# A hand-held issue order of 2640 steps, exchanged for another order of the same steps

## The chip, the cores and the metric

The kernel runs on one core of one Trainium2 chip. The metric is the device time of one execution in microseconds (us), the median over several runs; lower is better.

## The reference

The inputs are 16 batches of 256 query tokens x and 256 context tokens y, 256 features each, all in float32. Three attention layers with 16 heads of 16 features and one MLP are applied to every batch:

```python
# layer 0: cross attention with RMS norms, mask over the context
Q, K, V = rms(x, g_q) @ Wq, rms(y, g_c) @ Wk, rms(y, g_c) @ Wv      # by heads
x = rms(x + softmax(where(mask, Q K^T * scale, -inf)) V @ Wo, g_out)
# layer 1: causal self attention, layer norm, rotary turn of q and k
h = ln(x);  x = x + softmax(causal(rope(q) rope(k)^T)) v @ sa_wo + sa_bo
# layer 2: cross attention, q from ln(x), k and v from y, rotary turn
x = x + softmax(rope(q) rope(k)^T) v @ ca_wo + ca_bo
# MLP with 1024 hidden features
x = x + gelu(ln(x) @ fc1 + b1) @ fc2 + b2
```

## The kernel before

Work is cut into 48 attentions, one for each batch and layer. The list ORDER gives the layer of each: attentions 0 to 4 belong to layer 0, then the layers are mixed, and the last ones are of layer 2, so that batches are at different layers at the same time. Class Att holds the pieces of one attention as small methods; class Mlp holds those of the MLP for two batches. The methods are generators: each call goes to the next yield. A string PLAN lists which piece goes on next, and its order is the order in which instructions are put into the in-order queues of all engines:

```python
def step(word):
    if word not in steps:
        steps[word] = begin(word) or iter(())
    next(steps[word], None)
...
for word in PLAN.split():
    step(word)
```

A word is a method, the number of the attention and, for scores and values, a part. A word that stands three times is a generator in three stages. What the words mean, with lines as in the profile:

- `q.i`, `k.i`, `v.i`, `project.i`: a dense product of 32 column-tiled matmul records (L635 or L647) into one of three PSUM banks (tile d). The second stage reads the bank: DVE L796 (times rq, layer 0), ScalarE L762 (bias, layers 1 and 2), DVE L1076 or L1082 for project. For v the second stage is a small POOL instruction and the third the DVE read (L921 or L930). In layers 1 and 2 four further stages on DVE turn q and k (L770, L776 twice, an add).
- `k_high`, `k_low`, `k_out` and `q_high`, `q_low`, `q_out`: in layers 0 and 2 from attention 2 on ("fast"), q and k are split into two halves of float32r; k_high is ScalarE L877, q_high ScalarE L825, the low parts are DVE L881, L832 and L836, and the out steps are DMAs of SP (L889, L842).
- `scores.i.n`: the first stage is the matmuls (L966 fast, L955 else) into both buffers of tile S; the second and third are the two exponentials on ScalarE (L978), which free the two buffers. A causal attention has two more stages, masks on POOL (L986).
- `values.i.n`: the product with va into the single PSUM tile A (L1009); where a half of the heads is finished a second stage copies it (ScalarE, L1024). `take_last.i` is the copy of the last half.
- `heads_in`, `sums_in`, `invert` (three stages: DVE reciprocal, DMA to DRAM, DMA back), `divide` (POOL, then DVE L1069): the way from the copied result to `project`.
- `stats_x`, `stats_y`, `stats`, `norm`: normalization on DVE with a root on POOL. `send.i` and `receive.i` take the row factors of x through DRAM to tile rq (L719, L726 on SP). `pieces` and `pieces_in` turn a normalized batch through DRAM (L594, L600), `turn` does it with TensorE (L570).
- `load.b`, `load_early.n` (SP), `load_piece.b.n`, `load_later.n` (GpSimd's queue): loads of inputs and weights; load_early.0 is the first third of ca, 256 KB.
- `fold_of_att`, `fold_of_fc1`, `gain_*`, `combine.n`: work on the weights. `mlp.g.*`: the first MLP steps; mlp.0.up2 is a product whose PSUM result ScalarE copies (L1245).

The scores stage that sets how close two steps can stand:

```python
pss = [psS.tile([P, 2, 512], F32, tag="S", name="S") for g in range(2)]   # psS has 2 buffers
...                                      # 16 matmuls, alternating between the two tiles
for ps in pss:
    yield
    nc.scalar.activation(pt[:, :, :w], ps[:, :, :w], AF.Exp, scale=scale)
```

Before the plan a short written prologue runs attention 0's first products; after it, from about 672 us on, a written loop over the eight MLP groups runs to the end. Both are outside the string.

Of the kernel before, what the change touches and what calls it, by code (L numbers as in the profile page):

```python
# [55 lines left out]
scores.0.1 stats_x.2 values.0.0 q.1 scores.0.2 stats_y.2 v.1 scores.0.2 stats_y.2 scores.0.2  # L56
stats_x.3 values.0.1 load_piece.5.0 scores.0.3 stats_x.2 k.1 scores.0.3 stats_x.3 send.2 stats_y.3
scores.0.3 k.2 v.1 load_piece.5.1 v.1 send.2 k.1 values.0.1 send.3
scores.1.0 k_high.2 k_low.2 load_early.4 q.2 scores.1.0 send.3 scores.1.0 values.0.2 receive.2
load_early.3 scores.1.1 k_out.2 values.0.3 scores.1.1 q.3 q.2 scores.1.1 take_last.0 load_early.0  # L60
q_high.2 scores.1.2 q_low.2 values.1.0 scores.1.2 q_low.2 heads_in.0 v.2 v.2 stats_y.6 scores.1.2
q_out.2 scores.1.3 v.2 sums_in.0 k.3 stats_x.6 scores.1.3 receive.3 scores.1.3 load.4 values.1.1
k_high.3 values.1.1
scores.2.0 invert.0 values.1.2 k_low.3 scores.2.0 q.3 values.1.3 scores.2.0 heads_in.0 take_last.1
q_high.3 scores.2.1 invert.0 v.3 v.3 k_out.3 q_low.3 stats_x.6 scores.2.1 q_low.3 sums_in.1
scores.2.1 stats_y.3 values.2.0 stats_x.4 scores.2.2 stats_x.4 q_out.3 k.4 scores.2.2
load_piece.6.0 send.4 v.3 send.4 scores.2.2 load_piece.5.3 values.2.1 send.6 divide.0 k_high.4
stats_y.4 scores.2.3 invert.0 q.4 invert.1 scores.2.3 k_low.4 scores.2.3 receive.4 invert.1
stats_x.8 values.2.1
scores.3.0 heads_in.1 stats_x.8 values.2.2 scores.3.0 heads_in.1 fold_of_att load_piece.6.1  # L70
scores.3.0 q.4 load_early.2 load_later.1 values.2.3 divide.0 stats_y.4 q_high.4 invert.1
scores.3.1 send.8 take_last.2 project.0 scores.3.1 q_low.4 k_out.4 q_low.4 scores.3.1 values.3.0
project.0 fold_of_att q_out.4 scores.3.2 project.0 v.4 v.4 divide.1 scores.3.2 stats_y.8 project.0
scores.3.2 values.3.1 load_piece.5.2 finish.0 fold_of_att load_piece.7.2 scores.3.3 stats.5
values.3.1 k.6 scores.3.3 v.4 stats.5 scores.3.3 values.3.2 load_piece.7.0 sums_in.2 norm.5
k_high.6
scores.4.0 load_piece.7.1 k_low.6 values.3.3 scores.4.0 divide.1 fold_of_att turn.5 take_last.3
scores.4.0 send.6 project.1 fold_of_att turn.5 sums_in.3 invert.2 scores.4.1 heads_in.2 divide.2
project.1 load_later.0 q.5 project.1 scores.4.1 heads_in.2 fold_of_att project.1 scores.4.1
values.4.0 invert.2 invert.3 q.5 load_piece.6.2 scores.4.2 finish.1 heads_in.3 k.5 scores.4.2 q.5  # L80
q.5 load_early.1 scores.4.2 invert.3 values.4.1 q.5 receive.6 k.5 q.5 scores.4.3 k_out.6
values.4.1 q.6 k.5 q.5 q.5 invert.2 k.5 scores.4.3 v.5 v.5 stats_y.6 k.5 scores.4.3 k.5 heads_in.3
load_piece.6.3 values.4.2 q.6 stats.7
scores.5.0 q_high.6 values.4.3 stats.7 q_low.6 scores.5.0 v.6 q_low.6 scores.5.0 take_last.4
scores.5.0 q_out.6 divide.2 scores.5.0 send.8 scores.5.1 v.5 divide.3 v.6 norm.7 project.2
invert.3 scores.5.1 pieces.7 scores.5.1 pieces.7 scores.5.1 values.5.0 sums_in.4 project.2
scores.5.2 project.2 scores.5.1 k.8 v.6 scores.5.2 project.2 divide.3 pieces_in.7 scores.5.2
scores.5.2 values.5.1 finish.2 k_high.8 scores.5.2
scores.6.0 values.5.1 heads_in.4 project.3 load_later.6 stats.9 scores.6.0 load_piece.7.3 k_low.8
scores.6.0 stats.9 values.5.2 invert.4 stats_y.10 load_later.4 invert.4 scores.6.1 load_later.9  # L90
take_last.5 q.7 scores.6.1 norm.9 keep.5 pieces.9 scores.6.1 values.6.0 project.3 divide.4
sums_in.5 q.7 scores.6.2 project.3 pieces.9 k.7 q.7 scores.6.2 heads_in.4 project.3 q.7 scores.6.2
invert.4 values.6.1 q.7 q.7 scores.6.3 heads_in.5 q.7 v.7 k.7 invert.5 invert.5 divide.5
scores.6.3 k.7 receive.8 v.7 load_piece.9.0 heads_in.5 q.8 q.7 k.7 stats_y.8 values.6.1 k.7
scores.6.3 invert.5 values.6.2 k.7 divide.4 k_out.8
scores.7.0 v.7 project.4 stats_x.10 scores.7.0 pieces_in.9 q.8 scores.7.0 scores.7.0 values.6.3
project.4 q_high.8 load_piece.8.1 scores.7.1 divide.5 load_later.5 q_low.8 project.5 stats_x.10
scores.7.1 q_low.8 take_last.6 q_out.8 scores.7.1 scores.7.1 v.8 project.5 sums_in.6 stats.11
scores.7.0 scores.7.2 project.4 stats.11 q.9 scores.7.2 heads_in.6 scores.7.1 norm.11 scores.7.2
values.7.0 scores.7.2 pieces.11 q.9 values.7.1 load_piece.8.2  # L100
scores.8.0 pieces.11 q.9 values.7.1 v.8 k.10 scores.7.2 invert.6 scores.8.0 heads_in.6
load_later.8 q.9 scores.8.0 keep.9 q.9 values.7.2 k_high.10 invert.6 v.8 load_piece.8.0 scores.8.1
stats_y.10 take_last.7 scores.8.1 k.9 q.9 sums_in.7 scores.8.1 q.9 project.4 gain_ca values.8.0
k.9 finish.3 scores.8.2 send.10 v.9 v.9 k.9 divide.6 send.10 scores.8.2 load_later.7 k_low.10
invert.6 scores.8.2 invert.7 values.8.1 k.9 q.9 pieces_in.11 scores.8.3 k.9 values.8.1 k.11
finish.4 scores.8.3 receive.10 k.9 invert.7 scores.8.3 k_out.10 values.8.2 v.9 k.11 stats_x.14
scores.9.0 k.11 heads_in.7 stats_x.14 q.10 scores.9.0 k.11 load_later.10 invert.7 divide.6
scores.9.0 values.8.3 scores.9.0 q.10 heads_in.7 divide.7 scores.9.1 k.11 load_later.3 q_high.10
k.11 scores.9.0 project.6 scores.9.1 take_last.8 load_piece.9.1 q_low.10 k_high.11 sums_in.8 v.10
v.10 scores.9.1 stats.13 scores.9.1 q_low.10 scores.9.1 values.9.0 project.6 q_out.10 scores.9.2  # L110
send.14 divide.7 stats.13 heads_in.8 q.11 k_low.11 scores.9.2 load_piece.10.0 norm.13 heads_in.8
scores.9.2 scores.9.2 invert.8 project.7 v.10 q.11 keep.7 invert.8 q.11 values.9.1 scores.9.2
k_out.11
scores.10.0 q.11 values.9.1 k.12 scores.10.0 q.11 project.7 scores.10.0 values.9.2 q.11 invert.8
stats.12 q_high.11 scores.10.1 heads_in.9 v.11 v.11 take_last.9 stats.12 scores.10.1 pieces.13
sums_in.9 scores.10.1 q_low.11 values.10.0 norm.12 k.12 scores.10.2 pieces.13 q_low.11 keep.12
turn.12 stats.16 q_out.11 scores.10.2 fold_of_fc1 load_piece.8.3 v.11 heads_in.9 scores.10.2
values.10.1 divide.8 k.12 stats.16 turn.12 scores.10.3 invert.9 values.10.1 divide.8 q.12 divide.9
scores.10.3 k.12 pieces_in.13 k.12 scores.10.3 values.10.2 k.12 invert.9 q.12
scores.11.0 stats_y.14 project.8 q.12 scores.11.0 q.12 scores.11.0 values.10.3 q.12 fold_of_fc1  # L120
k_high.12 q.12 scores.11.1 fold_of_fc1 take_last.10 k.13 scores.11.1 k_low.12 invert.9 project.8
scores.11.1 k_out.12 values.11.0 q_high.12 scores.11.2 v.12 v.12 q_low.12 fold_of_fc1 scores.11.2
q_low.12 scores.11.2 divide.9 q_out.12 values.11.1 norm.16 k.13 scores.11.3 project.6 heads_in.10
project.9 scores.11.3 k.13 project.6 send.14 k.13 values.11.1 load_later.2 scores.11.3 k.14
sums_in.10 k.13 stats_y.14 project.9 k.13
scores.12.0 load_piece.10.1 v.12 values.11.2 scores.12.0 gain_fc1.0 stats.15 values.11.3
scores.12.0 pieces.16 k_high.14 receive.14 scores.12.1 pieces.16 k_low.14 q.13 scores.12.1
heads_in.10 stats.15 take_last.11 project.8 scores.12.1 keep.11 values.12.0 sums_in.11 invert.10
q.13 scores.12.2 load_piece.10.2 invert.10 q.13 values.12.1 scores.12.2 divide.10 q.13 v.13 v.13
heads_in.11 scores.12.2 q.13 q.13 values.12.1 heads_in.11 scores.12.3 q.13 q.13 norm.15 q.14  # L130
invert.10 scores.12.3 pieces.15 scores.12.3 finish.6 pieces.15 values.12.2 k_out.14 q.14
scores.13.0 invert.11 stats_x.17 divide.11 k.15 invert.11 scores.13.0 stats.19 pieces_in.15
scores.13.0 scores.13.0 values.12.3 v.13 q_high.14 stats.19 scores.13.1 k.15 stats_x.17 q_low.14
v.14 scores.13.1 divide.10 q_low.14 scores.13.1 scores.13.1 take_last.12 project.10 k.15 q_out.14
# [1932 lines left out]
```

## Time and profile before

| | |
|---|---|
| median of 3 runs | 880.16 us (880.13 to 881.4) |
| the profiled execution's own time | 880.08 us |
| its span, first to last instruction | 878.4 us |
| instructions | 32887 |
| busy: PE, PE weight load, DVE, ACT, POOL | 99%, 64%, 75%, 68%, 40% |
| DMA: bytes, mean rate | 107.04 MB, 122 GB/s |
| granted TensorE clock | 1.000 |

PE is TensorE, PEld its weight loads, DVE VectorE, ACT ScalarE, POOL GpSimd, SP the engine that issues most DMAs. A line of the timeline gives the start in us, the length in us, engine, line, operation, the tile written and those read, and the number of records merged; in brackets stand the idle time before and what ended it. A line of the waits gives who waited for whom, the total in us, how often, and the longest. The busy time of PE is modelled at its end, so a wait of a few tenths of a microsecond can lie hidden in it.

### The profile page before, as it was taken

The page shows a single profiled execution, that of the slowest core. Times are in us where ns is not written, and L with a number is a line of the kernel's source. Part 1 is how long each engine was busy: PE and PEld are TensorE (multiplying, and loading weights), DVE is VectorE, ACT ScalarE, POOL GpSimd, SP SyncE. Part 2 cuts the span into 40 slices and gives each one's busy share as a digit, 9 for nine tenths or more (in the row PEclk, how much of TensorE's full clock was granted, in tenths as well). Part 3 has the DMA queues.
Part 4 walks back from the last instruction along what each step waited for, and adds up shares of the span by engine and source line. Part 5 has one row for each costly group of instructions (what it writes and reads, how often), then busy time and mean ns, then how long its engine had stood idle before and what let it go on. Part 6 is the DMA issues. An engine that isn't in the chain of part 4 may idle for free.

```text
span 878.4 us, 32887 instructions
## 1 busy us (share of the span) xinstructions
PE 867.9 (99%) x13762; PEld 558.9 (64%) x13762; DVE 660.0 (75%) x1487; ACT 593.4 (68%) x848; POOL 352.9 (40%) x558
## 2 busy tenths in 40 slices
PE   8999999999999999999999999999999999999997
PEld 4455555555555555555555555555556899999997
DVE  5368888888787878788776788888784787787562
ACT  4788767877787877788777787788876733333440
POOL 4154685257355357264555534334152132222000
PEclk9999999999999999999999999999999999999999
DMA  8576465455344345443343333224331022211201
GB/s 275 182 225 189 134 182 178 148 164 167 117 153 131 110 138 169 144 132 118 126 134 125 113 115 131 95 83 155 124 110 52 14 72 73 67 55 30 69 25 51
DMA packets 101454, 107.04 MB, mean 122 GB/s; under 512 B 26602, under 2 KB 81778, under 8 KB 101298
## 3 DMA queue, kind: packets, MB, share of 16 engines
q1 hardware_dynamic: 96210, 89.89, 31.1%
q0 software_dynamic: 4400, 14.42, 5.6%
q8 instruction: 110, 1.80, 0.9%
q10 hardware_dynamic: 688, 0.54, 0.2%
q14 instruction: 46, 0.38, 0.1%
HBM read 46.33 MB, written 13.65 MB: 68 GB/s over the span
## 4 chain that ended last, share of the span: by engine, by line
PE 86%; DVE 4%; DMA 3%; issue 2%; SPq 2%; ACT 2%; POOL 1%; ACTq 0%; DVEq 0%; POOLq 0%
PE d L647 17%; PE d L635 16%; PE A L1009 15%; PE S L966 8%; PE upX L1223 6%; PE S L955 6%; PE A L1321 6%; PE downZ L1321 3%; PE upZ L1223 3%; PE d L1321 2%; PE d L1223 2%; ACT pt L978 1%; PE d L570 1%; PE downX L1321 1%; DMA hT<-turn_hop 1%
## 5 line engine op out<-in xcount | busy, mean ns | idle before, releaser
L978 ACT ACTIVATE pt<-S 128x1024 f32<-128x1024 f32 x224 | 218.6, 1025 | 87.7 <-PE S L955 56.5
L1009 PE MATMUL A<-pt,va 128*32 128x256 f32 (+1 forms) x3072 | 183.1, 362 | 0.1
L978 ACT ACTIVATE pt<-S,sy 128x1024 f32<-128x1024 f32 x128 | 137.0, 1116 | 28.6 <-PE S L966 16.1
L1009 PEld LDWEIGHTS A<-pt,va 128*32 128x32 f32 x3072 | 94.3, 110 | 63.9 <-issue 7.4
L986 POOL TENSOR_SCALAR_AFFINE_SELECT pt<-pt 128x512 f32<-128x512 f32 x128 | 94.4, 757 | 77.3 <-ACT pt L978 76.7
L966 PEld LDWEIGHTS S<-qm,kT 32*128 32x128 f32 x1920 | 66.6, 183 | 49.6 <-issue 23.6
L966 PE MATMUL S<-qm,kT 32*128 32x256 f32 x1920 | 92.6, 303 | 1.5 <-ACT pt L978 1.3
L623 POOL TENSOR_TENSOR cur<-cur,bias 128x512 f32<-128x512 f32 x48 | 63.8, 1334 | 39.4 <-DVE xn L555 39.2
L527 POOL TENSOR_SCALAR r_ln<-bmv 128x2 f32<-128x2 f32 x48 | 15.6, 325 | 138.5 <-DVE bmv L546 137.4
L1024 ACT COPY av<-A 128x512 f32<-128x512 f32 x96 | 56.6, 590 | 20.6 <-PE A L1009 20.4
L1245 ACT COPY g<-upX 128x512 f32<-128x512 f32 x28 | 15.0, 589 | 72.4 <-issue 68.1
L955 PE MATMUL S<-qm,kT 32*64 32x512 f32 (+1 forms) x1152 | 63.5, 512 | 0.0
L635 PE MATMUL d<-hT,sa 128*32 128x256 f32 x1024 | 61.4, 381 | 0.4 <-DMA hT<-turn_hop 0.4
L762 ACT ACTIVATE a<-d,qk_bias 128x256 f32<-128x256 f32 x128 | 53.9, 477 | 4.6 <-PE d L635 4.4
L555 DVE TENSOR_SCALAR xn<-cur,bmv,r_ln 128x256 f32<-128x256 f32 x96 | 49.2, 561 | 5.3 <-POOL r_ln L528 5.3
L776 DVE TENSOR_TENSOR a<-a,turn 128x512 f32<-128x512 f32 x64 | 48.5, 758 | 1.6
L1261 ACT ACTIVATE g<-g,fb 128x256 f32<-128x256 f32 x96 | 41.0, 499 | 11.1 <-DVE g L1250 11.1
L776 DVE TENSOR_TENSOR u<-u,turn 128x512 f32<-128x512 f32 x64 | 47.8, 747 | 0.0
L770 DVE STREAM_SHUFFLE u<-a 128x512 f32<-128x512 f32 x64 | 47.4, 740 | 0.3 <-issue 0.2
L635 PEld LDWEIGHTS d<-hT,sa 128*32 128x32 f32 x1024 | 30.8, 109 | 24.0 <-issue 3.4
L1069 DVE TENSOR_TENSOR oT<-oT,inv 128x512 f32<-128x512 f32 x48 | 35.9, 749 | 11.3 <-issue 5.5
L1067 POOL TENSOR_TENSOR seen<-seen,sums 128x64 f32<-128x64 f32 x48 | 19.4, 404 | 57.2 <-DVE sums L1053 50.6
(175 smaller groups left out, 1667.7 us busy)
## 6 DMA issues: line engine op xcount, KB each, us to landing
kT<-hl SPq DMA_DIRECT2D x60, 256.0 KB
qm<-qm SPq DMA_DIRECT2D x60, 256.0 KB
oT<-av SPq DMA_DIRECT2D x192, 64.0 KB
inv<-inv_hop SPq DMA_DIRECT2D x96, 128.0 KB
turn_hop<-bits SPq DMA_DIRECT2D x33, 256.0 KB
hT<-turn_hop SPq DMA_DIRECT2D x92, 64.0 KB
out<-res SPq DMA_DIRECT2D x15, 256.0 KB
cur<-in_x POOLq DMA_DIRECT2D x11, 256.0 KB, 3.5
```

Source lines behind the costliest of these rows:

```text
L623: nc.gpsimd.tensor_tensor(t, t, bias_sb[:, row : row + D].unsqueeze(1).to_broadcast([P, NC, D]), ALU.add)
L635: nc.tensor.matmul(o, lhsT=w[:, k, at + t * P + j : at + t * P + j + 32], rhs=tokens, start=(k == 0), stop=(k == KC - 1), skip_group_check ...
L647: nc.tensor.matmul(ps[j : j + 32, c * D : (c + 1) * D], lhsT=some_tokens(src, k, c, j), rhs=w[:, k, at : at + D], start=(k == 0), stop=(k ...
L776: nc.vector.tensor_tensor(t, t, table.unsqueeze(1).to_broadcast([P, KC, S]), ALU.mult)
L955: nc.tensor.matmul(ps[64 * half : 64 * half + 64, 2 * m * u : 2 * m * (u + 1)] .rearrange("p (i s) -> p i s", i=2), lhsT=self.kT[r, t, at] ...
L966: nc.tensor.matmul(ps[:, at : at + m], lhsT=self.kd[r, i, t, kc * P : (kc + 1) * P].bitcast(F32R), rhs=self.qd[r, i, h, t, q0:S].bitcast(F ...
L978: nc.scalar.activation(pt[:, :, :w], ps[:, :, :w], AF.Exp, scale=scale)
L986: nc.gpsimd.affine_select(out=diag, in_=diag, compare_op=ALU.is_ge, fill=0.0, base=0, pattern=[[0, 2], [0, 2], [1, P]], channel_multiplier=-1,
L1009: nc.tensor.matmul(self.av[32 * r : 32 * r + 32, i, q0:S], lhsT=self.va[:, kc, 8 * t + 2 * r + i, :], rhs=pts[r // 2][:, r % 2, i * m : (i ...
L1024: copy(av, self.av)
L1223: nc.tensor.matmul(o if len(b.shape) == 2 else by_groups(o), lhsT=a[:, c * P : (c + 1) * P], rhs=b, start=(first and c % 2 == 0), stop=Tru ...
L1321: nc.tensor.matmul(ps[:, c, :], lhsT=a[f // 2][:, f % 2, c * P : (c + 1) * P], rhs=b[:, f, :], start=(first and c == 0 and f == 0), stop=True,
```

## The change

The string PLAN is replaced by another order of the same words: all 2640 words occur in both, each equally often. The new order was chosen by a planner for the mean over five drawn sets of durations and transfer delays. Nothing else in the file differs. The parts of the diff that the text below comes to (line breaks in the string have no meaning):

```diff
-scores.1.0 k_high.2 k_low.2 load_early.4 q.2 scores.1.0 send.3 scores.1.0 values.0.2 receive.2
-load_early.3 scores.1.1 k_out.2 values.0.3 scores.1.1 q.3 q.2 scores.1.1 take_last.0 load_early.0
-q_high.2 scores.1.2 q_low.2 values.1.0 scores.1.2 q_low.2 heads_in.0 v.2 v.2 stats_y.6 scores.1.2
-q_out.2 scores.1.3 v.2 sums_in.0 k.3 stats_x.6 scores.1.3 receive.3 scores.1.3 load.4 values.1.1
-k_high.3 values.1.1
-scores.2.0 invert.0 values.1.2 k_low.3 scores.2.0 q.3 values.1.3 scores.2.0 heads_in.0 take_last.1
-q_high.3 scores.2.1 invert.0 v.3 v.3 k_out.3 q_low.3 stats_x.6 scores.2.1 q_low.3 sums_in.1
...
-load_piece.6.0 send.4 v.3 send.4 scores.2.2 load_piece.5.3 values.2.1 send.6 divide.0 k_high.4
-stats_y.4 scores.2.3 invert.0 q.4 invert.1 scores.2.3 k_low.4 scores.2.3 receive.4 invert.1
-stats_x.8 values.2.1
-scores.3.0 heads_in.1 stats_x.8 values.2.2 scores.3.0 heads_in.1 fold_of_att load_piece.6.1
-scores.3.0 q.4 load_early.2 load_later.1 values.2.3 divide.0 stats_y.4 q_high.4 invert.1
-scores.3.1 send.8 take_last.2 project.0 scores.3.1 q_low.4 k_out.4 q_low.4 scores.3.1 values.3.0
...
+scores.1.0 load_early.0 k_high.2 k_low.2 q.2 load_piece.5.1 send.3 scores.1.0 scores.1.0
+values.0.2 receive.2 load_early.3 scores.1.1 heads_in.0 q.3 scores.1.1 q.2 scores.1.1 values.0.3
+k_out.2 q_high.2 scores.1.2 take_last.0 q_low.2 v.2 v.2 scores.1.2 q_low.2 receive.3 scores.1.2
+q_out.2 values.1.0 scores.1.3 sums_in.0 k.3 scores.1.3 q.3 load.4 stats_y.6 scores.1.3 values.1.1
+stats_x.6 k_high.3
+scores.2.0 q_high.3 invert.0 k_low.3 values.1.1 scores.2.0 invert.0 q_low.3 values.1.2 v.2
+scores.2.0 values.1.3 k_out.3 take_last.1 scores.2.1 heads_in.0 q_low.3 v.3 scores.2.1 stats_x.4
...
+send.4 scores.2.2 load_piece.7.0 scores.2.2 divide.0 fold_of_att invert.0 k_high.4 scores.2.3
+k_low.4 heads_in.1 q.4 scores.2.3 invert.1 receive.4 stats_x.8 scores.2.3 invert.1 load_early.2
+values.2.1 stats_y.4 k_out.4 stats_x.8
+scores.3.0 values.2.1 stats_y.4 scores.3.0 values.2.2 q.4 heads_in.1 values.2.3 divide.0
+scores.3.0 stats_x.6 send.8 q_high.4 load_piece.5.3 scores.3.1 send.6 take_last.2 send.6 project.0
...
-scores.9.2 scores.9.2 invert.8 project.7 v.10 q.11 keep.7 invert.8 q.11 values.9.1 scores.9.2
-k_out.11
-scores.10.0 q.11 values.9.1 k.12 scores.10.0 q.11 project.7 scores.10.0 values.9.2 q.11 invert.8
...
+stats.13 heads_in.8 scores.9.2 divide.7 q.11 keep.7 v.10 heads_in.8 invert.8 project.7 scores.9.2
+q.11 norm.13 invert.8 load_later.2 q.11 k_out.11 scores.9.2 values.9.1
+scores.10.0 project.7 divide.8 values.9.1 k.12 q.11 scores.10.0 q.11 scores.10.0 q.11 values.9.2
...
-invert.44 q.47 scores.45.3 k.47 mlp.0.stats scores.45.3 k.47 values.45.1 k.47
-scores.46.0 q.47 k.47 values.45.2 divide.44 scores.46.0 q.47 values.45.3 scores.46.0 divide.44
...
-scores.46.3 invert.45 values.46.1 scores.46.3 mlp.0.turn project.43 heads_in.45 keep.45
-values.46.2 v.47 heads_in.45 mlp.0.turn
-scores.47.0 mlp.0.turn mlp.1.stats invert.45 scores.47.0 values.46.3 scores.47.0 take_last.46
-scores.47.1 mlp.1.stats sums_in.46 mlp.0.up2 scores.47.1 heads_in.46 scores.47.1 divide.45
...
+mlp.0.stats scores.45.3 turn.47 invert.44 divide.44 values.45.1 keep.44 scores.45.3 q.47
+scores.45.3 k.47 k.47 values.45.1
+scores.46.0 k.47 q.47 values.45.2 k.47 scores.46.0 q.47 values.45.3 scores.46.0 divide.44
...
+scores.47.0 heads_in.45 mlp.0.turn scores.47.0 mlp.1.stats values.46.3 invert.45 mlp.0.turn
+scores.47.0 mlp.0.turn project.43 heads_in.46 scores.47.1 take_last.46 keep.45 mlp.0.turn
+sums_in.46 mlp.0.up2 scores.47.1 keep.46 scores.47.1 divide.45 values.47.0 mlp.0.keep scores.47.2
```

## The prediction

> **What bounds the kernel now.** I read the page first, for which engine is full and where.
>
> ```profile
> span 878.4 us, 32887 instructions
> ...
> PE 867.9 (99%) x13762; PEld 558.9 (64%) x13762; DVE 660.0 (75%) x1487; ACT 593.4 (68%) x848; POOL 352.9 (40%) x558
> ...
> PE   8999999999999999999999999999999999999997
> ...
> PEclk9999999999999999999999999999999999999999
> DMA  8576465455344345443343333224331022211201
> ```
>
> TensorE is busy in all of the span but the first and last slices, at full clock; no other engine passes 75%. The change adds and removes no instruction, so TensorE's own work is fixed and only its waits can move. The waits by engine show almost none for PE:
>
> ```profile
> PE S L966 <- ACT pt L978: 1.3, 3, 0.6
> PE d L635 <- DMA hT<-turn_hop: 0.4, 1, 0.4
> PE d L635 <- DVE va L921: 0.4, 1, 0.4
> PE d L570 <- DVE xn L555: 0.4, 2, 0.2
> PE d L647 <- DVE oT L1069: 0.3, 1, 0.3
> ```
>
> A modelled matmul end hides short waits, so I went to the timeline of PE and took starts: the time from a group's start to the next group's start is the same to some 0.02 us for the same pair of groups all through the run (S of L966 then d: 0.68; d then A: 1.75; A then S: 0.98), and what exceeds it is a wait. Two of them:
>
> ```profile
> 41.57 0.75 PE L966 MATMUL S<-qm,kT 32*128 32x256 f32 x16
> 42.35 1.93 PE L1009 MATMUL A<-pt,va 128*32 128x256 f32 x32
> 44.22 1.13 PE L966 MATMUL S<-qm,kT 32*128 32x256 f32 x16
> 45.28 1.93 PE L647 MATMUL d<-w,yT 128*32 128x256 f32 x32
> ...
> 53.99 1.20 PE L966 MATMUL S<-qm,kT 32*128 32x256 f32 x16
> 55.13 1.07 PE L1009 MATMUL A<-pt,va 128*32 128x256 f32 x16
> ```
>
> 45.28 - 44.22 is 1.06 for 0.68 (0.39 with unrounded starts); 55.13 - 53.99 is 1.14 (0.46 lost). Listed over the whole run past the start: 0.39 (44), 0.46 (54), 0.52 (119, hT's DMA), 0.48 (152, DVE late with va), 0.33 (228, oT), 0.43 (506, xn), 0.23 (638, xn), 0.21 (643), 0.50 (646), 0.56 (659), 0.69 and 0.91 (663 and 664, ScalarE behind mlp.0.up2). The sum is 5.7 us: the most that any order of the planned part can save. After some 672 us the plan has ended, and nothing changes there.
>
> **The limit that the order has to respect.** Each scores step fills both S buffers, and its matmuls need both exponentials of the step before. The exponentials take 2.12 us a pair in layer 0 and 1.94 in the others, S itself 0.68 to 0.74, and about 0.12 passes before ScalarE starts. So two scores must lie 3.0 us (layer 0) or 2.75 us apart on PE, plus what ScalarE has to do between the two exponentials or, over 0.7 us, ahead of them. I counted this for the 176 steps in both orders, with 1.75 for a dense group, 0.93 for A, 0.70 or 1.06 for S.
>
> **The change part by part.** The sum is made against the profiled execution's own 880.08 us (878.4 of span and 1.7 around it); the median is 880.16. All 2640 words of the plan are in both orders, each as often, so there is no work to add or take away; the terms are places.
>
> What it takes away:
> - 54 us: between scores.2.3 and scores.3.0 stood 2.45 us of PE work; now the product of values.2.1 stands there too (it stood one step earlier), and it is 3.38, over 3.0. Saves 0.46.
> - 152 us: k.12 needed the PSUM bank that v.10's last step (DVE, L921) reads, and 1.14 us of PE work lay between them in the plan while DVE waited for sums; now 2.89. Saves 0.48.
> - 643 us: scores.45.3 to scores.46.0 goes from 2.45 to 3.38 (values.45.1 now between): saves 0.21. It also leaves ScalarE less behind at scores.46.1, whose own gap stays 2.56: half of 0.50, so 0.25.
> - 659 us: scores.47.0 to scores.47.1 goes from 2.22 to 2.81 (both transposes of mlp.0.turn now stand between, before one): saves 0.56.
> Sum 1.96.
>
> What stays: pieces_in.7 to q.7 is 4.96 us in both orders (0.52), up2 stands between scores.47.1 and scores.47.2 in both (0.69 and 0.91). At 228 inv.12 is issued 5.01 instead of 6.76 us ahead of project.12; but DVE waited there until 228.28, long after that transfer of 2.83 from 221.74, so I leave 0.33 as it is.
>
> What it brings:
> - 44 us: q_high.3 (L825, 1.07) now stands in ScalarE's queue before the exponentials of scores.2.0, as do k_high.3 (0.58) and av (0.59). The rows of before for this stretch:
>
> ```profile
> 39.05 2.12 ACT L978 ACTIVATE pt<-S,sy 128x1024 f32<-128x1024 f32 x2 [1.65 <-PE S L955]
> 41.06 0.58 ACT L877 CAST hl<-d 128x512 fp32r<-128x512 f32 x1
> 41.71 0.59 ACT L1024 COPY av<-A 128x512 f32<-128x512 f32 x1
> 42.44 2.12 ACT L978 ACTIVATE pt<-S,sy 128x1024 f32<-128x1024 f32 x2
> 44.45 0.59 ACT L1024 COPY av<-A 128x512 f32<-128x512 f32 x1
> 44.91 1.07 ACT L825 CAST qm<-qa 128x1024 fp32r<-128x1024 f32 x1
> ```
>
> The exponentials then start at 41.7 + 1.07 + 0.59 = 43.4 instead of 42.44: scores.2.1 waits 0.95 longer.
> - 55 to 60 us: scores.3.0 to 3.1 falls from 3.46 to 2.56, 0.4 under its limit, and the next step has q_high.4 and take_last.2 (1.66) in a period of 3.38, where 3.78 is asked for: between 0.4 and 1.07, I take 0.6.
> - 38 us: the DMA of ca's Wq (256 KB, load_early.0) moves ahead of rq.2's on SP, and q_high.2 ahead of take_last.0 on ScalarE. In before DVE waited for rq.2:
>
> ```profile
> 32.85 0.69 DVE L796 TENSOR_TENSOR qa<-d,rq 128x512 f32<-128x512 f32 x1 [4.92 <-DMA rq<-rq_hop]
> ```
>
> It had been issued at 26.92, 5.93 earlier. If it lands L later, q_high.2 and the exponentials of scores.1.2 behind it slip, and scores.1.3 loses L - 0.45: 0.1 because ScalarE is at exponentials until 33.6, 0.35 because those of scores.1.2 ended 0.35 before they were needed. At the 182 GB/s of that slice 256 KB take 1.44, which would cost 1.0; none if the transfers share the queue without delay. I take 0.4.
> - Elsewhere: some small new shortfalls (scores.20.2, 28.1, 39.x) of 0.1 to 0.5 each by the count, most of which earlier slack hid in before: 0 to 0.8, I take 0.3.
> Sum 2.25.
>
> Here a rule of the Trainium skill can be held against the row. "DMA: Bandwidth & Descriptors", section "Anatomy of one DMA", gives about 2.0 us fixed and bytes over 436 GB/s for a transfer issued by GpSimd; by it 256 KB would add an estimated 0.6 to L (0.15 at scores.1.3), and rq.2's 128 KB would take 2.3. The row's 5.93 for rq.2, on another queue, says that this stretch is not described by it.
>
> Net +0.3: 880.08 + 0.3 = 880.4. With no new wait and all of the savings it would be 878.1; with all of the upper prices (0.95 + 1.07 + 1.0 + 0.8 = 3.8) and half of the savings 882.9. The DMA queue of SP and POOL's are reordered throughout; I counted how much PE work lies between each transfer and its user, and the thin places are mostly wider than in before (send to receive at least 2.07 us after 1.63, q_out to scores at least 3.38 after 3.04). I cost them at nothing, PE work covering them; where a cover fails, one such wait costs 0.3 to 0.5 (the rows at 119 and 152).
>
> **The rivals.** (1) Faster: the wider places act and the new ones do not. Then the 1.96 go, and with them the single DMA and DVE waits at 119, 228 and 506 (0.52, 0.33, 0.43): 880.08 - 3.2 = 876.8. For it: the count of steps under the exponential limit sums to 5.2 us in the new order after 6.7 in the old. Against: it overstates, since of the 6.7 only 2.1 were seen (44, 54, 643, 646, 659), and three of the largest new ones stand where DMA is busiest (DMA 8, 5, 7 tenths in the first slices).
> (2) Slower, one mechanism: rq.2 lands late behind ca's weights, ScalarE's in-order queue holds q_high.2 in front of the exponentials, and PE stops at scores.1.3. L could reach 5.9, if the new transfer ahead takes as long as rq.2's own did. At L = 3 it costs 2.5 instead of the 0.4 taken, and the kernel takes 882.5; with the upper price at 55 to 60 us 883.0. It decides from L = 2.4 on.
> (3) The order does what it was chosen for only under drawn durations, and this chip's agree with the old ones to 0.02 us: then nothing is gained. That is the forecast's own reading.
>
> **How the numbers follow.** About 0.2% (1.76 us) is what can be told from no change, so no change is 878.4 to 881.9. The forecast, 880.4, gets 0.40; faster at about 876.8 gets 0.26; slower at about 883 gets 0.34. The forecast's own range is 878.1 to 882.9. For 8 in 10 I go down to 876.8 and up to 883.6, half a microsecond past the slow rival for waits that no row shows.
>
> **What would show it.** PE's starts: S at 44 with about 1.6 us to the next group instead of 1.06; no lost time at 54, 152 and 659; scores.1.3 at 38 with the next group on time, and DVE's qa of batch 2 no later than 34.3. I am wrong if qa comes after 35.3 (rival 2), if the planned part ends before 670 us (rival 1), or if PE loses more than 1 us in one place that is not named here.

## The result and the profile after

The new order is faster: 878.2 us, the median of 20 runs, beside 881.0 for 20 runs of the old order in the same series; the ratio is 0.9974, its 95% interval 0.9965 to 0.9983. That is 2.3 us (1.5 to 3.1), where no change was forecast. The profiled execution took 878.07 us against 880.08. Since the old order's median moves between 879.9 and 881.0 from one series of runs to the next, only ratios within a series are compared below.

The page, in the lines that answer to those shown of before:

```profile
span 876.3 us, 32875 instructions
...
PE 865.1 (99%) x13762; PEld 557.4 (64%) x13762; DVE 664.0 (76%) x1487; ACT 592.5 (68%) x848; POOL 349.4 (40%) x558
...
DMA  8666466454353354343444323324331022211201
```

TensorE does the same 13762 products at the same share. The new order has 12 instructions fewer, all of them semaphore instructions; of every other kind there are as many as before. The 2.1 us of span is too little to see here, and so it is in the waits of PE:

```profile
PE A L1009 <- ACT av L1024: 1.6, 2, 0.8
PE S L966 <- ACT pt L978: 1.1, 2, 0.6
```

Of the five lines shown of before, those for hT, va and xn are gone, those for oT and the exponentials (pt) smaller; a new one leads, ScalarE's copy of A, two waits of 0.8. The places come from PE's starts, as in the prediction. First the two stretches at 42 and 58 us:

```profile
41.86 0.75 PE L966 MATMUL S<-qm,kT 32*128 32x256 f32 x16
43.42 1.93 PE L1009 MATMUL A<-pt,va 128*32 128x256 f32 x32 [0.81 <-ACT av L1024]
45.29 0.89 PE L966 MATMUL S<-qm,kT 32*128 32x256 f32 x16
...
58.28 1.13 PE L966 MATMUL S<-qm,kT 32*128 32x256 f32 x16
59.34 1.93 PE L647 MATMUL d<-w0o,oT 128*32 128x256 f32 x32
```

43.42 - 41.86 is 1.56 where the pair S, A takes 0.68 (0.88 lost); 59.34 - 58.28 is 1.06 for 0.68 (0.39 lost). What stood before the copy is seen on ScalarE: q_high.3 (L825), then av, a place that the new order chose.

```profile
41.82 1.07 ACT L825 CAST qm<-qa 128x1024 fp32r<-128x1024 f32 x1
42.76 0.61 ACT L1024 COPY av<-A 128x512 f32<-128x512 f32 x1
```

The second new wait is at 248 us and was not foreseen. The lines of the timeline around it:

```profile
242.35 3.00 POOL L986 TENSOR_SCALAR_AFFINE_SELECT pt<-pt 128x512 f32<-128x512 f32 x5
242.91 3.05 DVE L776 TENSOR_TENSOR u<-u,turn 128x512 f32<-128x512 f32 x1
246.00 2.05 DVE L865 TENSOR_TENSOR hl<-a,u 128x512 f32<-128x512 f32 x1
248.17 0.84 ACT L762 ACTIVATE a<-d,qk_bias 128x256 f32<-128x256 f32 x2 [1.50 <-DVE hl L865]
...
251.06 1.29 PE L1009 MATMUL A<-pt,va 128*32 128x128 f32 x28 [0.77 <-ACT av L1024]
```

Read downwards: POOL runs five masks without a gap; DVE's step of k.18, 0.69 us elsewhere, takes 3.05 under them, and the next 2.05; ScalarE waits 1.50 for the end of that one, which reads the tile a that ScalarE writes next; the copy of A behind it is late; PE loses 0.92 (2.68 from the product's start at 248.38 to 251.06, for 1.76).

For all that follows I made the list of lost times for each profile: every place where the time between two starts of PE exceeds the usual one of that pair by more than 0.09 us, "usual" being the median over the profiles.

### The profile page after: what moved, and what is told of

Read it like the earlier page. It is cut to its first block, busy times and chain, and to the rows that moved or that the text cites. A ratio compares the mean times of both kernels' runs of the same rounds, so it can differ in the third digit from the quotient of the medians.

```text
span 876.3 us, 32875 instructions
## 1 busy us (share of the span) xinstructions
PE 865.1 (99%) x13762; PEld 557.4 (64%) x13762; DVE 664.0 (76%) x1487; ACT 592.5 (68%) x848; POOL 349.4 (40%) x558
## 4 chain that ended last, share of the span: by engine, by line
PE 91%; DVE 4%; ACT 1%; DMA 1%; SPq 1%; issue 1%; POOL 1%; ACTq 0%; DVEq 0%; POOLq 0%
PE d L647 18%; PE d L635 18%; PE A L1009 17%; PE S L966 9%; PE upX L1223 6%; PE S L955 6%; PE A L1321 6%; PE downZ L1321 3%; PE upZ L1223 3%; PE d L1321 2%; PE d L1223 2%; PE d L570 1%; PE downX L1321 1%; ACT pt L978 1%; DMA hT<-turn_hop 1%
## 5 line engine op out<-in xcount | busy, mean ns | idle before, releaser
L986 POOL TENSOR_SCALAR_AFFINE_SELECT pt<-pt 128x512 f32<-128x512 f32 x128 | 88.6, 715 | 53.9 <-ACT pt L978 53.3
L623 POOL TENSOR_TENSOR cur<-cur,bias 128x512 f32<-128x512 f32 x48 | 63.6, 1329 | 32.6 <-DVE xn L555 32.5
L1245 ACT COPY g<-upX 128x512 f32<-128x512 f32 x28 | 15.0, 589 | 72.4 <-issue 68.1
L635 PE MATMUL d<-hT,sa 128*32 128x256 f32 x1024 | 61.4, 381 | 0.0
L776 DVE TENSOR_TENSOR a<-a,turn 128x512 f32<-128x512 f32 x64 | 47.0, 735 | 1.6
L776 DVE TENSOR_TENSOR u<-u,turn 128x512 f32<-128x512 f32 x64 | 48.0, 750 | 0.0
L1067 POOL TENSOR_TENSOR seen<-seen,sums 128x64 f32<-128x64 f32 x48 | 19.3, 403 | 69.3 <-DVE sums L1053 67.2
L555 DVE TENSOR_SCALAR xn<-cur,bmv,r_ln 128x256 f32<-128x256 f32 x96 | 44.8, 516 | 2.5 <-POOL r_ln L528 2.3
L1069 DVE TENSOR_TENSOR oT<-oT,inv 128x512 f32<-128x512 f32 x48 | 36.1, 752 | 6.8 <-DMA hT<-turn_hop 2.3
```

The costliest lines, as they stand in the source:

```text
L623: nc.gpsimd.tensor_tensor(t, t, bias_sb[:, row : row + D].unsqueeze(1).to_broadcast([P, NC, D]), ALU.add)
L635: nc.tensor.matmul(o, lhsT=w[:, k, at + t * P + j : at + t * P + j + 32], rhs=tokens, start=(k == 0), stop=(k == KC - 1), skip_group_check ...
L776: nc.vector.tensor_tensor(t, t, table.unsqueeze(1).to_broadcast([P, KC, S]), ALU.mult)
L986: nc.gpsimd.affine_select(out=diag, in_=diag, compare_op=ALU.is_ge, fill=0.0, base=0, pattern=[[0, 2], [0, 2], [1, P]], channel_multiplier=-1,
```

## The experiments

All kernels differ only in the string. The first four divide it: an order up to a step, and of the words that are left the other order.

**Parts of the order.**

```text
 e1_early          new order up to the first scores.4.0, then the old order of the rest
 e2_mid            old up to scores.4.0, new up to scores.45.0, then old
 e3_end            old up to scores.45.0, then new
 e4_all_but_early  old up to scores.4.0, then new
```

> The new order up to the word before scores.4.0 (the first 65 us), then the old order of all that is left. Theory P (each loss belongs to a place in the order, so the parts add up): scores.4.0 starts 0.85 us later, with the waits of 0.88 at 42 and 0.39 at 58, and the old order's losses at 119, 228 and 506 come back: 0.7 to 0.9 us slower than before. Theory F (the forecast's own terms: 0.95 + 0.6 + 0.4 - 0.46): 1.5 us slower. Theory V (the rest is the luck of an execution: transfers land now early, now late): 0.8 slower, within what executions of the old order differ among themselves.

> The old order up to scores.4.0, the new one from there to scores.45.0 (65 to 640 us), then the old order again. Theory P: the middle was worth -1.5 us by the starts of scores.4.0 (+0.85) and scores.45.0 (-0.65) in the two profiled executions, so 1.5 us faster than before, with the wait of 0.92 at 248 in it and none at 119, 152, 228 and 506. Theory F: -0.48 at 152 and +0.3 elsewhere, 0.2 faster. Theory V: the waits at 119, 228 and 506 come and go with the execution and not with the order, so about 0.5 faster (152 alone).

> The old order up to scores.45.0, then the new one to the end of the plan. Theory P: scores.45.0 to the end of the execution is 1.4 us shorter in the new order (losses at 638, 643, 646 and 659), so 1.4 us faster than before. Theory F: 0.21 + 0.25 + 0.56 = 1.0 faster. Theory V: 0.8 faster (643 and 659, which ScalarE's order sets; 638 varies).

> The old order up to scores.4.0, then the new one to the end. Theory P: the sum of the middle and the end, 2.9 us faster than before and 0.85 faster than the whole new order. Theory F: 1.2 faster than before and 1.5 faster than the whole new order. Theory V: 1.3 faster than before.

Measured, as ratios to the old order in the same series with their intervals: early 0.9999 (0.9990 to 1.0009), mid 0.9992 (0.9983 to 1.0001), end 0.9999 (0.9988 to 1.0009), all but early 0.9980 (0.9971 to 0.9989). So the end alone does not bring the 1.4 us that theory P asked for, and all but early brings 1.8 of the 2.9 that it expected. The early part shows none of the 0.7 to 1.5 us that the three theories wanted (its interval ends at 0.8), although its two waits (0.88 and 0.39) are in its profile. The parts (-0.1, -0.7 and -0.1 us by the ratios) sum to less than 2.3, but each is known to some 0.9 us only, so the times alone do not show that parts fail to add. The profiles show more. e3_end has the old order up to 629 us, yet in its profile the losses at 119, 152, 160 and 228 were all missing: they are not places of the order. And its end was 1.06 us longer after the last product, of which more below.

**The same order again.** Both kernels unchanged, two more executions of each.

> The old order once more, unchanged, for the profile of another execution. Theory P (each loss belongs to a place in the order): TensorE loses the same times at the same places, 0.52 at 119, 0.47 at 152, 0.27 at 160, 0.33 at 228 and 0.34 at 638 among them. Theory V (these places hang on how early a transfer lands, and differ between executions; those that ScalarE's queue makes do not): 0.38 at 44, 0.46 at 54, 0.43 at 506, 0.21 at 643, 0.50 at 646 and 0.57 at 659 recur to 0.05, and of the other five some are missing and new ones are there.

> The old order a third time. As for the second: theory P wants the same list, theory V the same six fixed places and another choice of the others.

> The new order once more, unchanged. Theory P: 0.88 at 42, 0.39 at 58, 0.92 at 248, 0.39 at 507 and 0.32 at 644, and nothing over 0.1 at 119, 152, 160, 228 and 638. Theory V: the first five recur; the second five stay small only if the new order leaves their transfers more room, and up to 1.5 us may come at one of them.

> The new order a third time. As for the second: theory P wants the same list in all three, theory V fixed places and places that come and go, fewer of these than in the old order if it is that which makes it faster.

The single times were 879.85 and 879.35 for the old order, 877.75 and 877.92 for the new one. Together with experiments that have the same order up to the end of a stretch, up to six profiles of one order can be set side by side. Lost times by stretch in us, each number one execution:

| stretch | old order | mean | new order | mean | new - old |
|---|---|---|---|---|---|
| 5 to 61 us | 0.94 1.47 0.94 1.31 1.40 | 1.21 | 1.51 1.50 1.52 1.52 1.52 1.67 | 1.54 | +0.33 |
| 61 to 231 | 1.98 1.71 0.98 0.29 1.99 | 1.39 | 0.53 0.28 0.91 0.29 0.54 1.08 | 0.61 | -0.78 |
| 231 to 630 | 1.84 1.83 1.82 1.83 1.81 | 1.83 | 2.05 2.06 2.04 2.04 | 2.05 | +0.22 |
| 630 to 671 | 3.22 3.23 3.22 | 3.22 | 2.02 2.00 2.02 2.03 | 2.02 | -1.20 |

(A loss of 0.25 at 61.0 us of e3_end stands in the first row, the same place at 61.4 and 61.5 of two others in the second.)

There are two kinds of loss. After 231 us the lists agree place by place to 0.02 us in every execution of an order: these are fixed. Between 61 and 231 us, where the DMA row of the page stands at 4 to 6 tenths, they come and go. Theory V had the right kind, but not the right list: 638 recurred in all executions with the old order there (0.23 and 0.11; 0.10 and 0.11 in e2_mid, with the new order ahead of it) and is fixed; 119 came with 0.52, 0, 0.43, 0 and 0.16, 152 with 0.47, 0.98, 0, 0 and 0.59, 228 only in the first. The new order's one restless place is 115 (0.24, 0, 0.62, 0, 0.25, 0.80; 1.38 in e2_mid).

How a delay of some tenths turns into a loss at 152: DVE at the same steps in the second execution of the old order, with PE's wait, and then in e3_end, which has the same order there:

```profile
149.03 3.38 DVE L555 TENSOR_SCALAR xn<-cur,bmv,r_ln 128x256 f32<-128x256 f32 x2
...
153.75 0.62 PE L635 MATMUL d<-yT,ca 128*32 128x256 f32 x6 [0.91 <-DVE va L921]
```

```profile
148.33 0.81 DVE L555 TENSOR_SCALAR xn<-cur,bmv,r_ln 128x256 f32<-128x256 f32 x2
...
149.52 0.90 DVE L921 TENSOR_SCALAR va<-d,r_y,mask 128x256 f32<-128x256 f32 x2
```

The same pair of steps takes 3.38 or 0.81. In both executions DVE had waited for oT's transfer just before; it came to this pair 0.7 us later in the first (0.4 against TensorE). There two POOL masks and the long POOL step L623 (1.28) ran beside its second half; in e3_end the pair was done as the first of these masks began. va follows 3.3 us later, and PE waits. So the last step of this loss is DVE beside POOL; what made DVE late is not settled by these rows.

**The two places that the new order brings, and one that it keeps.**

q_high.3 back behind take_last.1:

```diff
-scores.2.0 q_high.3 invert.0 k_low.3 values.1.1 scores.2.0 invert.0 q_low.3 values.1.2 v.2
-scores.2.0 values.1.3 k_out.3 take_last.1 scores.2.1
+scores.2.0 invert.0 k_low.3 values.1.1 scores.2.0 invert.0 values.1.2 v.2
+scores.2.0 values.1.3 k_out.3 take_last.1 q_high.3 q_low.3 scores.2.1
```

> The new order with q_high.3 (and the DVE step that follows it) put back behind take_last.1. Theory P (the 0.88 at 42 is ScalarE's queue: the copy of A stands behind q_high.3): the wait of 0.88 goes and the old order's 0.38 at 44 comes back, 0.14 at 45 goes: the planned part is 0.55 shorter than in the new order. Rival (the place is set by something else, S or the second half of values.1): 0.88 stays. A second rival: the gain is given back between 55 and 230 us, where waits come and go; then the loss at 42 goes but scores.17.0 starts no earlier.

The cause is shown: 0.88 became 0.10. But 0.14 at 45 became 0.39, 0.39 at 58 became 0.84 (a wait for DVE's oT, L1069) and a loss of 0.25 at 61 came: 0.78 gained and 0.95 given back in this execution, which looks like the second rival's case, only nearer than it said. It is not a fixed price, though: f4_three below has the same order up to 243 us, and there 58 lost 0.38 and 61 lost 0.16. The ratio was 0.9986 (0.9977 to 0.9994): no gain on the new order's 0.9974 is shown.

One mask moved on POOL:

```diff
 scores.16.1
-scores.16.0
 take_last.15 k.18 load_piece.11.0 sums_in.15 v.17 scores.16.1 norm.18
...
 scores.16.2 k.18 turn.18
-scores.16.0 k.18
+k.18 scores.16.0 scores.16.0
 scores.16.1 q.18
```

> The new order with one POOL mask, the first of scores.16.0, moved behind k.18's last step (DVE's and ScalarE's and TensorE's orders stay the same). Theory P (POOL's masks one after another keep DVE from finishing its step, which took 3.05 us for 0.69): POOL now waits for the exponentials of scores.16.1 until 243, DVE's step takes 0.7 to 1.3, and the wait of 0.92 at 248 goes: 0.9 shorter. Rival (DVE's step is long because of what it reads, or the profile shows its wait as work): 3.05 and 0.92 stay.

The loss at 248 went from 0.92 to nothing, and the rest of the fixed list did not move. The ratio was 0.9980 (0.9968 to 0.9992): the 0.9 us are seen in the profile, and not in these times beside the new order's 0.9974. DVE's two steps, whose own order and inputs are the same, and POOL's masks:

```profile
241.82 4.50 POOL L986 TENSOR_SCALAR_AFFINE_SELECT pt<-pt 128x512 f32<-128x512 f32 x6 [0.55 <-ACT pt L978]
242.30 0.72 DVE L776 TENSOR_TENSOR u<-u,turn 128x512 f32<-128x512 f32 x1
243.05 1.00 DVE L865 TENSOR_TENSOR hl<-a,u 128x512 f32<-128x512 f32 x1
```

3.05 and 2.05 became 0.72 and 1.00, though masks still run beside them. The single records show who yields: in the new order the second mask starts 0.04 us after DVE's step (242.95 and 242.91), takes its usual 0.65, and DVE waits to the end of the row; here it starts 0.13 us after it (242.43 and 242.30), takes 1.08, and DVE goes on. So it is not the overlap that costs DVE 2.4 us, but whose turn it is. The other profiles agree. Take every L776 that starts while POOL is at such a step (L986, L623, L1067) or within 0.1 us of its end: where the next of them starts less than 0.05 us after L776 (two places, at 243 and 380 us), DVE took 1.18 to 3.06 us in 12 of 13 cases; where it starts 0.1 to 0.3 us after it, in none of 83 was DVE over 1.0; where it starts 0.4 to 0.6 us after it, so that the running step has only begun, DVE was over 1.0 in 40 of 42.

mlp.0.up2 behind the exponentials of scores.47.1:

```diff
-sums_in.46 mlp.0.up2 scores.47.1 keep.46 scores.47.1 divide.45
+sums_in.46 scores.47.1 keep.46 scores.47.1 mlp.0.up2 divide.45
```

> The new order with mlp.0.up2 moved behind the two exponentials of scores.47.1, a place that both orders share with a loss of 0.69 + 0.91. Theory P: its two copies no longer stand ahead of the exponentials on ScalarE, and 1.5 us go. Rival: TensorE then waits for the copies elsewhere before 672 us, and 0.3 or less is won.

In the new order PE waits twice at scores.47.2 for exponentials that stand behind up2's copies (L1245); with the move the copies are behind the exponentials, and S follows A without a wait. New order, then f3_up2:

```profile
662.04 0.39 PE L966 MATMUL S<-qm,kT 32*128 32x256 f32 x2 [0.60 <-ACT pt L978]
662.95 0.73 PE L966 MATMUL S<-qm,kT 32*128 32x256 f32 x14 [0.53 <-ACT pt L978]
```

```profile
658.42 1.94 ACT L978 ACTIVATE pt<-S 128x1024 f32<-128x1024 f32 x2 [0.43 <-PE S L966]
660.25 1.08 ACT L1245 COPY g<-d 128x512 f32<-128x512 f32 x2
661.18 0.74 PE L966 MATMUL S<-qm,kT 32*128 32x256 f32 x16
```

All of the 0.70 + 0.90 went (2.02 to 0.41 lost after 630 us); the ratio was 0.9967 (0.9953 to 0.9980).

> The three changes together. If the losses are places, they add: 0.55 + 0.9 + 1.5 = 2.95 us less than the new order, a span of about 873.3 for 876.2, and 5 us or 0.6% less than before. If a later transfer takes back what an earlier place gives, less than 2.

The three together gave 0.9951 (0.9938 to 0.9963), 4.3 us under the old order, and a span of 874.0, 2.3 less than the new order's. By places the mask and up2 give their full 0.92 and 1.60, and from 41 to 62 us 1.13 was lost instead of 1.51; 1.39 was lost at 115 in this execution. Whether q_high.3 adds anything in the mean is open: g1_two below leaves it in place and has 0.9954.

**Are the restless losses crowded transfers?** The four loads of fc2 are not needed before the MLP, so they can leave the crowded stretch:

```text
-load_later.7, load_later.8, load_later.9, load_later.10 at 105 to 150 us
+one each behind the first scores.18.0, scores.19.0, scores.20.0, scores.21.0
```

> The new order with the mask of scores.16.0 and mlp.0.up2 moved, q_high.3 left where the new order has it. By the fixed places 0.92 + 1.6 = 2.5 us less than the new order: 0.55% less than before. Control for the next two.

> The same, with the four loads of fc2 (256 KB each on GpSimd's queue, load_later.7 to 10, not needed before the MLP) moved from 105-150 us to 262-305 us. Theory V (the losses from 61 to 230 us are late transfers, and the loads crowd them): the loss at 115, between 0 and 1.4 so far in the new order, is 0.1 or less, and the times lie 0.3 us lower and closer together than those of the control. Rival (the small transfers are slow by themselves): the same losses, no difference.

> The old order with nothing changed but those four loads, moved to the same part. Theory V: the losses at 115, 119, 152, 160 and 228 (1.7, 1.7, 1.0 and 0.25 in four executions) fall under 0.5 together, and the kernel is 0.8 us (0.1%) faster than before: then room for transfers is worth what the new order won there. Rival: unchanged within 0.05%.

> As the second, with the old order up to scores.4.0. By the fixed places the old beginning is 0.58 us shorter (0.94 lost against 1.52): 0.6 us less than the second if the transfers after it have room, and the same as the second if what the beginning wins is waited for between 61 and 230 us.

> The old order up to scores.4.0, the new one from there, with the mask of scores.16.0 and mlp.0.up2 moved and the loads of fc2 left in place. By fixed places 0.58 us less than the same without the old beginning (0.9954 of before), so 0.9947. If what the beginning wins is waited for between 61 and 230 us: 0.9954 again, with a loss of 0.5 or more at 115.

The control g1 gave 0.9954 (0.9940 to 0.9968). With the loads moved, the losses between 61 and 231 us were 0.29 (g2), 0.28 (g4; both only the fixed place at 184) and, on the old order, 0.72 (g3), against means of 0.61 and 1.39; but two of the six executions of the new order without the move, and one of the five of the old, had 0.28 or 0.29 too. g3's ratio, 0.9992 (0.9983 to 1.0001), lies where theory V put it, but its interval still holds no change. In the improved new order the times do not fall: 0.9959 (0.9945 to 0.9972), and 0.9956 (0.9942 to 0.9970) for g4, whose old beginning thus shows no 0.6 us. A loss that may be why is in both profiles: PE lost 0.69 and 0.74 at 279 us, where g1 lost nothing; fc2's second load was issued at 272 us, and DVE then waited 3.65 and 3.70 us for rq's transfer instead of 2.82. In g2's profile fc2's last load was issued at 298.26, hT's transfer at 303.55, and PE lost 2.12, 1.32 and 0.37 from 307 to 313 us; that execution took 879.86 us and the other four 875.75 to 877.42, so this is one execution's. So the loads have something to do with the waits where they stand, but that they alone make the restless losses is not shown.

The last of these, with the old beginning and the loads in place, is the best version run: 875.08 us beside 879.88, ratio 0.9943 (0.9931 to 0.9955). Its ratio is the expected 0.9947 rather than 0.9954, but the interval holds both. Its profile also lacks the 0.30 at 416 us. That loss is in all nine profiles with the new beginning and the new middle, and in none of the four with the old beginning and the new middle, though the words around 416 us are the same: a fixed loss can hang on an order some 350 us ahead of it. Why was not followed.

**The end of e3_end.**

> The old order up to scores.45.0 and the new end, once more. If the tail of 8.0 us after TensorE's last start (6.9 to 7.0 in every other profile) belongs to this kernel's code, it is there again and the times are within 0.3 us of before: 1.3 won and 1.06 lost. If it was one execution's, the tail is 6.9 and the times lie about 1.3 us (0.15%) under before.

It is that kernel's own: 7.97 us from the start of PE's last group to the end of the span here and 8.00 in e3_end, 6.89 to 7.02 in the 18 other profiles. The times were again those of before (0.9994, 0.9984 to 1.0004): 1.2 won by the places, 1.06 lost behind the last product. The last DVE step and the DMA queue of instructions in the last 20 us, e3_end (span 876.3) and then e4_all_but_early (span 875.6):

```profile
870.30 0.42 DVE L1338 TENSOR_TENSOR res<-downX,cur 128x256 f32<-128x256 f32 x1 [1.36 <-PE downX L1321]
...
q14 instruction: 4, 0.03, 0.6%
```

```profile
870.59 0.42 DVE L1338 TENSOR_TENSOR res<-downX,cur 128x256 f32<-128x256 f32 x1 [1.37 <-PE downX L1321]
...
q14 instruction: 3, 0.02, 0.4%
```

e3_end is ahead by 0.29 at its last computation and behind by 0.7 at the end, with one more load of instructions in between: four in the last 20 us, here and in the repeat, and three in the 18 other profiles. The written end is the same text in both; the page counts 32890 instructions in e3_end, 32887 in the old order and 32875 in the new one. That the additional load is what delays it was not tried.

## Why the prediction was wrong, step by step

**What bounds it: right, but the list was short.** TensorE, its waits, and the method of starts held: fixed places repeat to 0.02 us. That the change "adds and removes no instruction" holds for all but 12 semaphore instructions. The list named 5.7 us; at 0.09 and over it is 8.0. Missing were 160, 184, 280, 361 and 537 (0.27, 0.29, 0.32, 0.31, 0.26), which look like ordinary pairs one at a time, the smaller halves of 506 and 638, and five places of 0.10 to 0.13.

**What it takes away: right in size.** 54 fell from 0.46 to 0.10, 643 and 646 together from 0.71 to 0.32 (said 0.46 saved), 659 from 0.57 to nothing. 152 went too, but it was no fixed 0.48: of five executions of the old order it is in three.

**What stays: this step failed, and it decides the sign.** Fixed losses that were left in the sum, or not in it, went: 506 (0.17 + 0.43), 638 (0.23 + 0.11), 280 (0.32) and 537 (0.26), 1.52 in all. At 506 TensorE had waited for xn (DVE L555), and xn for the root on POOL (L528). Old order, then new:

```profile
502.07 2.25 POOL L986 TENSOR_SCALAR_AFFINE_SELECT pt<-pt 128x512 f32<-128x512 f32 x2
505.36 1.06 DVE L555 TENSOR_SCALAR xn<-cur,bmv,r_ln 128x256 f32<-128x256 f32 x2 [1.54 <-POOL r_ln L528]
```

```profile
499.96 2.86 POOL L986 TENSOR_SCALAR_AFFINE_SELECT pt<-pt 128x512 f32<-128x512 f32 x4 [2.14 <-ACT pt L978]
503.86 1.58 DVE L555 TENSOR_SCALAR xn<-cur,bmv,r_ln 128x256 f32<-128x256 f32 x2 [1.53 <-POOL r_ln L528]
```

In both orders the root stands behind four masks. In the old one a POOL step of divide (L1067, 0.31) stood between them, and three of the four took 1.08 to 1.21 us instead of 0.64 beside DVE steps; in the new one only one took 1.09, and the root is done 1.5 us earlier. No run moved these steps alone, and the waits at 280, 537 and 638 were not followed further. I had followed each wait to its nearest releaser, DVE or DMA, and asked how much TensorE work lies between; what the releaser itself stood behind, on POOL's queue, was counted nowhere, and the reordering of that queue was put at nothing. 119 and 228 belong to the executions, with means of 0.22 and 0.07 where 0.52 and 0.33 were carried on both sides. What was carried as unchanged on 61 to 231 us is 0.78 less in the mean.

**What it brings: right as a sum, wrong by place.** At 44 the price was 0.54 (0.88 + 0.14 after 0.10 + 0.38) instead of 0.95, and it fell on the copy of A behind q_high.3, not on scores.2.1. At 58 it was 0.39 for 0.6. At 38 nothing was lost: qa of batch 2 began at 31.19, earlier than before's 32.85, although ca's load was issued ahead; L was nothing or less. "Elsewhere", 0.3, was 1.61: 0.92 at 248, 0.39 at 507 and 0.30 at 416 (this one only with the new beginning). The first of these is POOL beside DVE, a resource that the count of ScalarE's periods cannot see, and whose rows were in the trace of before (DVE's L776 at 2.31 instead of 0.69 at 422 us, beside POOL's L623).

**The sum.** By the table the new order wins 1.4 us in the mean: +0.33 - 0.78 + 0.22 - 1.20. The forecast had +1.49, -0.48, +0.3 and -1.02 in the same stretches. The three profiled spans of each average 878.0 and 876.1, a difference of 1.9, and the measured 2.3 has 1.5 as its lower end. The rest is not placed: it can be in places under 0.09 us or in executions without a profile, and stays open.

**The rivals.** Rival 1 had the direction and named the places (119, 228, 506 go with the 1.96); that no new wait comes was wrong by 1.6 + 0.9 us, and only because unlisted losses went too is 876.8 no more than 1.3 under the profiled 878.07. Rival 2 is refuted by qa at 31.19: rq.2 landed 4.0 us after its issue, not 5.9. Rival 3, the forecast's own reading, failed in its premise: that this chip's durations agree to 0.02 us holds for computing steps, not for transfers between 61 and 231 us. There the old order lost between 0.29 and 1.99 us, the new one 0.28 to 1.08, which would fit an order chosen for a mean over drawn delays; these few executions do not show it. With the other profiles that have one or the other order from 65 to 231 us and the loads in place (e1_early 0.76; f1 0.71, f4 1.68, e2_mid 1.67, e4 0.60, g5 0.52) the means are 1.29 and 0.80. So 0.5 to 0.8 of the 2.3 us seem to be of this kind, and 1.2 is a better end.

**What would show it.** No loss at 152 and 659 and qa before 34.3 came true, and 54 nearly. S at 44 did not wait 1.6 (45.29 to the next start is 0.82); the planned part did not end before 670 (670.2).

## What to carry to other kernels

Take two or three profiles of the kernel before, and split its waits into those that recur to a few hundredths and those that come and go; price the first by place and the second by their mean, since one execution shows neither. When a new order is judged, follow each wait one step further than its releaser, on every queue that the releaser stands in, and mark where long POOL steps fall beside DVE. A gain in the plan can also be lost behind it: compare the time after the last product before a part is called worthless.

## What the runs showed of the hardware

**DVE beside POOL.** DVE's L776 took 3.05 us instead of 0.69 in all three executions of the new order, and 0.72 when one mask had been moved; in each of the first two profiles 40 DVE steps are over 0.4 us longer than their kind, all of them beside POOL steps. The Trainium skill's page "SBUF — State Buffer", section "SBUF: two separate sides", says that a DVE step with two inputs in SBUF, such as L776, and a GpSimd step that reads SBUF share a pair of ports by an exclusive lock, that whichever starts first has it for the whole instruction, and that the other blocks fully. The rows agree that it is a block and not a slowing. They add that a row of POOL steps can keep it: DVE waited through four masks of 0.65 us, not through one. By its start in the trace (242.91) it came ahead of these four, but under the end of a mask that was already running (242.35 to 243.02).

**Repeatability.** From 231 us to the end of the plan, each loss repeats to 0.02 us between executions of either order; between 61 and 231 us the sum differs by up to 1.7 us between executions of one order. With fc2's loads moved behind 231 us, one execution lost 3.8 us there. Which transfer makes the difference was not found.

**The end.** 1.06 us more after the last product, twice out of twice in one kernel and never in 18 profiles of others, with one more load of instructions; that this load is the cause was not tried.
